# The last group's sums over heads on two engines, p of the places on ScalarE, and the list of units among the one-hots

## The chip, the core and the metric

The kernel runs on one core of a Trainium2 chip. The metric is the device time of one execution in microseconds; the time of a kernel is the median of several executions. Engines are named as in the profile: PE (TensorE), DVE (VectorE), ACT (ScalarE), POOL (GpSimd) and SP, whose queue only issues transfers here.

## The reference

There are N = 6250 nodes with D = 256 features, 4 heads of 64 channels, 8 experts. The edges' sources and destinations come as `src` and `dst`; only the first N edges matter, because node n uses edge n.

```python
h = layernorm(x)
xt = (h @ weight).reshape(-1, 4, 64)
alpha = softmax(leaky_relu(al(xt[src]) + ar(xt[dst]), 0.01), axis=1)   # over the 4 heads
tmp = einsum('nh,nhd->nd', alpha[:N], xt[dst[:N]])                     # sum over heads
x = x + tile(tmp, 4)                                                   # the same 64 values for each head
tokens = layernorm(x)
probs = softmax(tokens @ router_w.T); the two largest, normalised to sum 1
for e in range(8):
    y = gelu(tokens @ w1[e] + b1[e]) @ w2[e] + b2[e]
    moe = tokens + sum of combine[:, e] * y
out = x + moe
```

## The kernel before

Nodes are laid on 128 partitions in NT = 49 tiles and worked on in five groups of 10, 10, 9, 10 and 10 tiles. For each group the kernel gathers the destinations' rows (`gather`, on POOL's queue), turns them on PE, multiplies them with the folded weights (`features`: 293 columns for each node, that is 4 heads of 72 columns, of which 64 are features and 8 are the heads' products with the router's rows), looks up the sources' terms (`look_up`), and makes the attention weights alpha (`attend_1`, `exponents`, `attend_2`).

`attend_3` is the sum over heads: a product of the 4 x 72 columns with alpha, an addition of two heads to the other two, and an addition of those two, the last one into the row of `xs[g]` that will be stored to a table in DRAM. `route` then takes the 8 router products, finds the best two experts of each node, stores the group's rows to the table (L605, SP's queue) and writes which of the 28 pairs of experts each node has (`mine_all`). `rank` and `ranked` count, on PE and DVE, the nodes of the same pair ahead of each node. For the first four groups these steps are spread by `tasks` between the matmuls of the next group; for the last group there is no next one, and they stand one after another.

After the last group follows a stage without loop. DVE adds up the counts (`ends`, `starts`, `base`), multiplies them out (`ms`) and gets each node's place in the order of pairs (`place_i`), split into a slice of 128 places and a lane in it (`slice_b`, `lane_b`). One-hot tables of both (`of_slice`, `of_lane`) and two weighted copies of the first (`by[:, 0]` with the partition number p, `by[:, 1]` with the tile number) go to 49 matmuls that sum into `pi`: for each place, which node stands there. This is done in three pieces of 10, 14 and 26 tiles (the 50th is padding). Then comes the list of units: a unit is an expert's work on a slice. `edge`, `has`, `member`, `takes`, `upto` and `every` find which experts each slice needs, a matmul `pu` numbers them, `unit` and `is_unit` make a one-hot of the numbers, and 16 matmuls `pf` make lists of slice and expert, from which the engines load registers (`which`, `for_act`, `for_pe`, `for_dve`). `held_by`, made from `pi`, says which rows the gathers from the table fetch (`fetch`, L939, POOL's queue). `keep_on` is a row of 26 matmuls whose result is not used.

The expert loop follows: 125 units, for each a load of w1 (`fill`), the first product (`first`, L1117), a gelu on ACT, the second product (`second`, L1133) and two additions into `acc` on DVE, with the layernorms (`norm`), transposes (`turn_slice`) and scattered stores of finished slices (`finish`) among them.

Each engine works through its instructions in program order, and the program is written out in the order in which they are to stand. Tiles of the pool `work` named with the tag `pxs` share two buffers in turn: the five groups' `pxs`, then `ms`, then `by`.

Of the kernel before, what the change touches and what calls it, by code (L numbers as in the profile page):

```python
# [9 lines left out]
FP = mybir.dt.float32  # L10
BF = mybir.dt.bfloat16
I32 = mybir.dt.int32
AF = mybir.ActivationFunctionType
ALU = mybir.AluOpType
# [8 lines left out]
def kernel(  # L23
# [37 lines left out]
    nc = tc.nc  # L61
    N, D = x.shape
    H, OC = attn_l.shape
    NE, _, F = w1.shape
    P = 128
    NT = -(-N // P)
# [17 lines left out]
    NPAIR = len(PATH)  # L84
    TS = 128
    NS = -(-N // TS)
# [3 lines left out]
    HB = OC + NE  # L90
    AR = H * HB
# [5 lines left out]
    U = D  # L97
# [11 lines left out]
    held = early.enter_context(tc.tile_pool(name="held", bufs=1))  # L109
# [4 lines left out]
    def wide(v, n):  # L114
        return v.rearrange("p (t k) -> p t k", k=1).to_broadcast([v.shape[0], v.shape[1], n])

    def long(v, n):
        return v.rearrange("p (t k) -> p t k", t=1).to_broadcast([v.shape[0], n, v.shape[1]])
# [12 lines left out]
    number = const.tile([128, 1], FP, name="number")  # L131
# [7 lines left out]
    xs = [held.tile([P, n, R], FP, name=f"x{g}") for g, (_, n) in enumerate(GROUPS)]  # L139
# [18 lines left out]
    mine_all = held.tile([P, NT, NPAIR], BF, name="mine_all")  # L158
    rank_all = held.tile([P, NT], FP, name="rank_all")
    outside = held.tile([P, 1], FP, name="outside")  # L160

    NTE = NT + NT % 2
    high_1 = held.tile([P, NTE * P], BF, name="high_1")
# [14 lines left out]
    work = early.enter_context(tc.tile_pool(name="work", bufs=2))  # L178
    small = early.enter_context(tc.tile_pool(name="small", bufs=2))
# [39 lines left out]
    for of, pattern, k in ((count_up, [[1, 128]], 0), (number, [[0, 1]], 1)):  # L219
        nc.gpsimd.iota(  # L220
            of, pattern=pattern, base=0, channel_multiplier=k,
# [160 lines left out]
    def pair_tables():  # L382

        nc.vector.tensor_scalar(before_b, count_up, number, None, ALU.is_gt)
        nc.vector.tensor_scalar(huge_b, ident, -HUGE, None, ALU.mult)
        nc.vector.tensor_scalar(valid, number, float(LAST), None, ALU.is_lt)

        nc.vector.tensor_scalar(
            outside, number, float(LAST), float(2 * NS * TS), ALU.is_ge, ALU.mult
        )  # L390


        for e in range(NE):
            nc.vector.memset(order[:, e : e + 1], 2.0 ** (NE - e))


        one_of = first_pool.tile([P, 2, NPAIR], FP, name="one_of")
        for i, (a, b) in enumerate(PATH):
            for k, e in enumerate((a, b)):
                nc.vector.memset(one_of[:, k, i : i + 1], float(e))  # L400
        for i, (a, b) in enumerate(PATH):
            nc.vector.memset(pairs[:, i : i + 1], 2.0 ** (NE - a) + 2.0 ** (NE - b))

        other = small.tile([NS, NE, NPAIR], FP, name="other", tag="mr", bufs=1)
        for k, to in enumerate((member, other)):
            nc.vector.tensor_tensor(
                to,
                one_of[:NS, k : k + 1, :].to_broadcast([NS, NE, NPAIR]),
                wide(count_up[:NS, :NE], NPAIR),
                ALU.is_equal,  # L410
            )
        nc.vector.tensor_tensor(member, member, other, ALU.add)

    def statistics(of, t0, n):
        stats = small.tile([P, n, 6], FP, name="stats", bufs=1)
        mv = small.tile([P, n, 2], FP, name="mv")
        for i in range(n):
            nc.vector.bn_stats(stats[:, i, :], of(t0 + i))
        for i in range(n):
            nc.vector.bn_aggr(mv[:, i, :], stats[:, i, :])  # L420
        return mv
# [52 lines left out]
    pxss, sqs, rstd_ds = {}, {}, {}  # L474
# [66 lines left out]
    def attend_2(g):  # L541

        ex, n = exs.pop(g), GROUPS[g][1]
        s = tiny("s", n)
        nc.vector.tensor_reduce(s, ex, AX.X, ALU.add)
        nc.vector.reciprocal(s, s)
        nc.vector.tensor_tensor(s, s, rstd_ds.pop(g), ALU.mult)
        alpha = small.tile([P, n, H], FP, name="alpha")
        nc.vector.tensor_tensor(alpha, ex, wide(s, H), ALU.mult)
        exs[g] = alpha  # L550

    def attend_3(g, i, n):

        at = slice(i, i + n)
        v = pxss[g][:, at, :AR].rearrange("p t (h k) -> p t h k", k=HB)
        nc.vector.tensor_tensor(
            v, v,
            exs[g][:, at, :].rearrange("p t (h k) -> p t h k", k=1)
            .to_broadcast([P, n, H, HB]), ALU.mult,
        )  # L560
        nc.vector.tensor_tensor(v[:, :, 0:2, :], v[:, :, 0:2, :], v[:, :, 2:4, :], ALU.add)
        nc.vector.tensor_tensor(
            xs[g][:, at, U : U + HB], v[:, :, 0, :], v[:, :, 1, :], ALU.add
        )


# [88 lines left out]
    def paced(t, n, of):  # L655

        nc.gpsimd.tensor_copy(pace[: of.shape[0]], of)
        for i in range(t, min(t + n, NT)):
            gather(i)

    fillers = {
        1: weights_columns,
        2: pair_tables,
        7: lambda: nc.vector.tensor_tensor(
            low_0[:, :NT, :], long(count_up[:, :NT], NT), wide(low, NT), ALU.not_equal
# [72 lines left out]
    def tasks(g):  # L738

        n = GROUPS[g][1]  # L740
        at = {i: [] for i in range(n)}

        def put(i, what):
            at[min(i, n - 1)].append(what)

        if g >= 1:
            f = g - 1
            m = GROUPS[f][1]
            put(1, lambda: attend_1(f))
            put(2, lambda: exponents(f))  # L750
            put(2, lambda: attend_2(f))
            for i in range(0, m, 3):
                put(3 + i // 3, lambda i=i: attend_3(f, i, min(3, m - i)))
            steps = route(f)
            for i in range(5):
                put(7 + i // 2, lambda: next(steps))
        if g >= 2:
            f2 = g - 2
            put(1, lambda: rank(f2))
            put(2, lambda: ranked(f2))  # L760
        if g == 3:
            put(0, load_experts)
        if g == 4:
            put(0, load_biases)
        return at

    at = {}
    for k, (g, b, n) in enumerate(FEATURES):
        if b == 0:
            at = tasks(g)  # L770
        after = None
        for j in range(n):
            i = b + j
            features(g, i, blocks, j)
            t = GROUPS[g][0] + i
# [19 lines left out]
    z = NG - 1  # L795
    n = GROUPS[z][1]
# [2 lines left out]
    rank(z - 1)  # L799
    ranked(z - 1)  # L800
    attend_2(z)
    attend_3(z, 0, n)
    steps = route(z)
    for _ in steps:
        pass
# [18 lines left out]
    nc.vector.tensor_tensor(starts, ends, count, ALU.subtract)  # L824
    base = small.tile([P, NG, NPAIR], FP, name="base", bufs=1)
    nc.vector.tensor_tensor(base, counts[:, :NG, :], long(starts, NG), ALU.add)
    ms = work.tile([P, NT, NPAIR], FP, name="ms", tag="pxs")
    for g in range(NG):
        nc.vector.tensor_tensor(
            ms[:, group(g), :], mine_all[:, group(g), :],  # L830
# [17 lines left out]
    slice_b, lane_b = parts  # L848

    pi = ps.tile([TS, 2, NS], FP, name="pi", tag="px")  # L850
    of_lane = held.tile([P, TS, NTE], BF, name="of_lane", tag="high_1")
    of_slice = held.tile([P, NS, NTE], BF, name="of_slice", tag="low_0")
    by = work.tile([P, 2, NS, NTE], BF, name="by", tag="pxs")

    for t0, t1 in ((0, 10), (10, 24), (24, NTE)):
        at, n = slice(t0, t1), t1 - t0
        for to, k, of in ((of_lane, TS, lane_b), (of_slice, NS, slice_b)):
            nc.vector.tensor_tensor(
                to[:, :, at], steps_b[:, :k, :n], long(of[:, at], k), ALU.is_equal
            )  # L860
        nc.vector.tensor_scalar(
            by[:, 0, :, at], of_slice[:, :, at], number, None, ALU.mult
        )
        nc.vector.tensor_tensor(
            by[:, 1, :, at], of_slice[:, :, at], long(count_b[:, at], NS), ALU.mult
        )
        for t in range(t0, min(t1, NT)):
            nc.tensor.matmul(
                pi, of_lane[:, :, t], by[:, :, :, t], start=(t == 0), stop=(t == NT - 1)
            )  # L870

    edge = small.tile([NS, 2], FP, name="edge", bufs=1)
    for k in range(2):
        nc.vector.tensor_scalar(
            edge[:, k : k + 1], number[:NS], float(TS), float(k * TS), ALU.mult, ALU.add
        )
    has = small.tile([NS, NPAIR], FP, name="has", bufs=1)
    nc.vector.tensor_scalar(has, ends[:NS], edge[:, 0:1], None, ALU.is_gt)
    nc.vector.scalar_tensor_tensor(
# [11 lines left out]
    nc.vector.tensor_copy(every, upto[:, NE - 1 :])  # L891
    pu = ps.tile([NS, 1], FP, name="pu", tag="r")
    nc.tensor.matmul(pu, before_b[:NS, :NS], every, start=True, stop=True)


    fields = small.tile([NS, 2, NE], BF, name="fields", bufs=1)
# [270 lines left out]
    for u in range(NU + LAG + 1):  # L1167
# [11 lines left out]
        k, step = divmod(u, 4)  # L1179
# [46 lines left out]
```

## Time and profile before

| | us |
|---|---|
| median of 3 executions | 432.43 (431.76 to 432.58) |
| the profiled execution | 430.84 |
| its span in the trace | 429.1 |
| PE busy in the span | 368.8 |
| DVE busy | 312.5 |
| ACT busy | 226.0 |
| POOL busy | 199.9 |

A line of the timeline gives the start and the duration in us, the engine, the line of the kernel, the operation, the tile written and the tiles read, their sizes (partitions x elements for each partition) and how many instructions were merged; in brackets stands the idle time of the engine ahead of it and what ended it. A line of groups gives the total busy time and the mean in ns after the first bar. "POOLq" or "SPq" is an engine's queue of commands. In the page's rows over the span, a digit is the busy share of one fortieth of the span in tenths, and PEclk the clock that PE was granted in the same unit.

### The profile page before, as it was taken

How to read it: one execution, taken by the hardware profiler on the slowest of the kernel's cores; microseconds unless marked ns; L12 is line 12 of the kernel's file. 1: busy time of each engine (PE TensorE's matmuls, PEld its weight loads, DVE VectorE, ACT ScalarE, POOL GpSimd, SP SyncE). 2: the span in 40 equal slices, each digit the busy share in tenths (PEclk: the TensorE clock that was granted, in tenths of full speed). 3: DMA queues.
4: the chain of work that ended last, by engine and by line, in shares of the span. 5: the costliest groups of instructions: out<-in, count | busy, mean ns of one | idle time of the engine just before them, and what ended most of it. 6: DMA issues, size and time to landing. Idle time of an engine off the chain costs nothing.

```text
span 429.1 us, 9886 instructions
## 1 busy us (share of the span) xinstructions
PE 368.8 (86%) x2575; PEld 320.0 (75%) x2575; DVE 312.5 (73%) x1092; ACT 226.0 (53%) x658; POOL 199.9 (47%) x240
## 2 busy tenths in 40 slices
PE   5798599888992127979999999999999999999990
PEld 4676388777881115469999999999998899999990
DVE  5999525897988896548778778877876877555551
ACT  3486279575762000057666666667665666333330
POOL 0068888888202000573343567667656633233222
PEclk9699699999997555799999999999999999999997
DMA  7974232446663110766667677777777765666610
GB/s 218 354 236 135 74 105 73 162 168 191 210 227 162 80 80 0 215 185 164 196 178 197 188 233 219 212 224 235 216 217 196 202 192 180 190 186 186 177 69 23
DMA packets 53896, 74.63 MB, mean 174 GB/s; under 512 B 7686, under 2 KB 48250, under 8 KB 52948
## 3 DMA queue, kind: packets, MB, share of 16 engines
q1 hardware_dynamic: 46028, 52.45, 39.9%
q0 software_dynamic: 7248, 21.29, 16.6%
q8 instruction: 23, 0.38, 0.4%
q10 hardware_dynamic: 568, 0.27, 0.3%
q14 instruction: 29, 0.24, 0.2%
HBM read 59.13 MB, written 14.87 MB: 172 GB/s over the span
## 4 chain that ended last, share of the span: by engine, by line
PE 49%; POOL 2%; issue 2%; ACT 1%; DVE 1%; POOLq 0%; ACTq 0%; DVEq 0%
PE ph L1117 24%; PE py L1133 23%; PE pt L1063 2%; POOL xr L939 1%; POOL nm L1020 1%; ACT hid L1124 0%; POOLq L1221 0%; DVE acc L1140 0%; DVE stats L1014 0%; ACT tok L1030 0%; ACTq L1077 0%; ACT acc L1040 0%; POOL out_dram L1144 0%; ACT tokT L1064 0%; POOL mv L1019 0%
## 5 line engine op out<-in xcount | busy, mean ns | idle before, releaser
L1117 PEld LDWEIGHTS ph<-tokT,w 128*128 128x128 f32 x1000 | 130.2, 191 | 13.8 <-ACT tokT L1064 7.7
L1117 PE MATMUL ph<-tokT,w 128*128 (+1 forms) x1000 | 132.5, 276 | 4.8 <-ACT tokT L1064 4.6
L1133 PE MATMUL py<-big,hid 128*128 x500 | 128.6, 380 | 0.0
L1124 ACT ACTIVATE hid<-ph,b_cols 128x128 f32<-128x128 f32 x250 | 77.9, 363 | 75.4 <-PE ph L1117 74.2
L1133 PEld LDWEIGHTS py<-big,hid 128*128 128x128 f32 x500 | 85.4, 191 | 7.0 <-DVE acc L1140 0.2
L939 POOL DMA_INDIRECT xr<-table,held_by x49 | 49.6, 1013 | 72.7 <-DVE held_by L913 39.2
L1140 DVE SCALAR_TENSOR_TENSOR acc<-py,shares,acc 128x256 f32 (+1 forms) x125 | 60.5, 484 | 28.0 <-PE py L1133 17.3
L1144 POOL DMA_INDIRECT out_dram<-acc,held_out x49 | 50.9, 1038 | 55.4 <-DVE acc L1140 39.2
L1140 DVE SCALAR_TENSOR_TENSOR acc<-big,shares,acc (+1 forms) x125 | 60.2, 481 | 11.3 <-issue 6.1
L1030 ACT ACTIVATE tok<-xr,nm 128x256 f32<-128x256 f32 x49 | 29.3, 599 | 60.9 <-DMA w<-in_L_ffn_w_dram 42.2
L480 PE MATMUL px<-w_sb,tT 128*128 128x293 f32 x196 | 56.6, 420 | 0.0
L480 PEld LDWEIGHTS px<-w_sb,tT 128*128 128x128 f32 x196 | 35.0, 194 | 7.3 <-issue 0.3
L236 POOL DMA_INDIRECT big<-in_x_dram,dst_sb x31 | 34.3, 1107 | 7.2 <-issue 6.8
L488 ACT COPY pxs<-px 128x293 f32<-128x293 f32 x49 | 19.8, 404 | 27.6 <-PE px L480 25.3
L251 ACT COPY tT<-pt 128x512 f32<-128x512 f32 (+2 forms) x56 | 26.9, 527 | 9.3 <-PE pt L247 8.9
L1004 DVE TENSOR_TENSOR xr<-xr 128x512 f32<-128x512 f32 (+1 forms) x25 | 17.2, 688 | 17.0 <-issue 17.0
L1040 ACT ACTIVATE acc<-xr,nm 128x256 f32<-128x256 f32 x49 | 29.1, 597 | 0.0
L509 PE MATMUL pl<-al_sb,high 128*128 128x196 bf16 x147 | 19.4, 250 | 8.0 <-DVE al_sb L464 5.9
L509 PEld LDWEIGHTS <-high 128*128 128x128 bf16 x147 | 13.6, 98 | 13.8 <-issue 6.1
L517 DVE TENSOR_REDUCE ag<-pl 128x8 f32<-128x392 f32 (+1 forms) x25 | 13.8, 551 | 11.8 <-PE pl L513 11.8
L1019 POOL TENSOR_SCALAR mv<-mv 128x2 f32<-128x2 f32 (+1 forms) x25 | 5.7, 229 | 35.0 <-DVE mv L1016 33.3
L236 POOL DMA_INDIRECT xd_own<-in_x_dram,dst_sb x18 | 18.5, 1027 | 4.4 <-issue 2.7
(217 smaller groups left out, 478.2 us busy)
## 6 DMA issues: line engine op xcount, KB each, us to landing
w<-in_L_ffn_w_dram SPq DMA_DIRECT2D x125, 256.0 KB
table<-x SPq DMA_DIRECT2D x4, 1685.0 KB
x<-in_x_dram SPq DMA_DIRECT2D x10, 512.0 KB
big<-in_L_ffn_w_dram SPq DMA_DIRECT2D x2, 1024.0 KB
high<-highs SPq DMA_DIRECT2D x1, 1568.0 KB
table<-x SPq DMA_DIRECT2D x1, 1516.5 KB
big<-in_L_ffn_b_dram SPq DMA_DIRECT2D x1, 1024.0 KB
xr<-table,held_by POOLq DMA_INDIRECT x49
```

The lines of the kernel that those rows point to most:

```text
L236: nc.gpsimd.indirect_dma_start(out=xd(t), out_offset=None, in_=x[:, :], in_offset=bass.IndirectOffsetOnAxis(ap=dst_sb[:, t : t + 1], axis=0),)
L251: nc.scalar.copy(tT, pt)
L480: nc.tensor.matmul(px, blocks[c][:, k * P : (k + 1) * P], w_sb[:, c, :], start=(c == 0), stop=(c == DC - 1),)
L509: nc.tensor.matmul(pl[:, k, :, :], high_1[:, t * P : (t + 1) * P], al_sb[:, part, :, :], start=(part == 0), stop=False,)
L939: nc.gpsimd.indirect_dma_start(out=xr[:, i, :], out_offset=None, in_=table[:, :], in_offset=bass.IndirectOffsetOnAxis(ap=held_by[:, s0 + i ...
L1030: nc.scalar.activation(tok[:, i, :], xr[:, i, :D], AF.Identity, bias=bias[:, i : i + 1], scale=scale[:, i : i + 1],)
L1040: nc.scalar.activation(acc[:, s * D : (s + 1) * D], xr[:, i, :D], AF.Identity, bias=bias[:, i : i + 1], scale=more[:, i : i + 1],)
L1117: nc.tensor.matmul(ph[:, j, :], w[:, c * F + j * 128 : c * F + (j + 1) * 128], tokT[:, bass.ds(rows_at + c * TS, TS)], start=(c == 0), sto ...
L1124: nc.scalar.activation(hid[:, j, :], ph[:, j, :], AF.Gelu, bias=b1_cols[:, :, j][:, bass.ds(at_act[u][0], 1)])
L1133: nc.tensor.matmul(py, hid[:, j, :], we2[:, j, bass.ds(at_pe[u][1], D)], start=(j == 0), stop=(j == FC - 1),)
L1140: nc.vector.scalar_tensor_tensor(to, y, share, to, op0=ALU.mult, op1=ALU.add)
L1144: nc.gpsimd.indirect_dma_start(out=ends_at[s][:, :], out_offset=bass.IndirectOffsetOnAxis(ap=held_out[:n, s : s + 1], axis=0), in_=acc[:n, ...
```

## The change

There are four edits. The last group's sums over heads are made in two parts: the 8 columns of router products on DVE, and then the 64 feature columns on GpSimd, with the same three operations each. `by[:, 0]` is made by an ACT instruction in place of a DVE one, and `of_slice` is made ahead of `of_lane`. The pieces of the one-hots are 8, 16 and 26 tiles; the list of units from `has` to the matmul `pu` stands between the second and the third piece, in place of behind the third. The two `edge` instructions move into `pair_tables`, near the start of the kernel, and `ms` gets the buffer of `x1` (group 1's rows), so that `by` takes the buffer that `ms` had and the last group's `pxs` stays in place.

```diff
-    def attend_3(g, i, n):
+    def attend_3(g, i, n, engine=nc.vector, k0=0, k1=HB):
         at = slice(i, i + n)
-        v = pxss[g][:, at, :AR].rearrange("p t (h k) -> p t h k", k=HB)
-        nc.vector.tensor_tensor(
+        v = pxss[g][:, at, :AR].rearrange("p t (h k) -> p t h k", k=HB)[:, :, :, k0:k1]
+        engine.tensor_tensor(
             v, v,
             exs[g][:, at, :].rearrange("p t (h k) -> p t h k", k=1)
-            .to_broadcast([P, n, H, HB]), ALU.mult,
-        )
-        nc.vector.tensor_tensor(v[:, :, 0:2, :], v[:, :, 0:2, :], v[:, :, 2:4, :], ALU.add)
-        nc.vector.tensor_tensor(
-            xs[g][:, at, U : U + HB], v[:, :, 0, :], v[:, :, 1, :], ALU.add
+            .to_broadcast([P, n, H, k1 - k0]), ALU.mult,
+        )
+        engine.tensor_tensor(v[:, :, 0:2, :], v[:, :, 0:2, :], v[:, :, 2:4, :], ALU.add)
+        engine.tensor_tensor(
+            xs[g][:, at, U + k0 : U + k1], v[:, :, 0, :], v[:, :, 1, :], ALU.add
         )
...
     attend_2(z)
-    attend_3(z, 0, n)
+    attend_3(z, 0, n, nc.vector, OC, HB)
+    attend_3(z, 0, n, nc.gpsimd, 0, OC)
     steps = route(z)
...
-    ms = work.tile([P, NT, NPAIR], FP, name="ms", tag="pxs")
+    ms = held.tile([P, NT, NPAIR], FP, name="ms", tag="x1")
...
-    for t0, t1 in ((0, 10), (10, 24), (24, NTE)):
+    def places(t0, t1):
         at, n = slice(t0, t1), t1 - t0
-        for to, k, of in ((of_lane, TS, lane_b), (of_slice, NS, slice_b)):
+        for to, k, of in ((of_slice, NS, slice_b), (of_lane, TS, lane_b)):
             nc.vector.tensor_tensor(
                 to[:, :, at], steps_b[:, :k, :n], long(of[:, at], k), ALU.is_equal
             )
-        nc.vector.tensor_scalar(
-            by[:, 0, :, at], of_slice[:, :, at], number, None, ALU.mult
-        )
+        nc.scalar.activation(by[:, 0, :, at], of_slice[:, :, at], AF.Identity, scale=number)
...
-    edge = small.tile([NS, 2], FP, name="edge", bufs=1)
-    for k in range(2):
-        nc.vector.tensor_scalar(
-            edge[:, k : k + 1], number[:NS], float(TS), float(k * TS), ALU.mult, ALU.add
-        )
+    places(0, 8)
+    places(8, 24)
     has = small.tile([NS, NPAIR], FP, name="has", bufs=1)
...
     nc.tensor.matmul(pu, before_b[:NS, :NS], every, start=True, stop=True)
+    places(24, NTE)
```

More of the change, by code (lines that the diff above doesn't have):

```diff
@@ L160 @@
     outside = held.tile([P, 1], FP, name="outside")
+    edge = held.tile([NS, 2], FP, name="edge")
     NTE = NT + NT % 2
@@ L412, in pair_tables @@
         nc.vector.tensor_tensor(member, member, other, ALU.add)
+        for k in range(2):
+            nc.vector.tensor_scalar(
+                edge[:, k : k + 1], number[:NS], float(TS), float(k * TS), ALU.mult, ALU.add
+            )
     def statistics(of, t0, n):
```

## The prediction

> **What bounds the kernel now.** I read the page first (where each engine is busy over the span), then the timeline between 138 and 182 us, which is the stage that the change touches, then the waits of that stage, and last the timeline around the few GpSimd instructions that read SBUF.
>
> ```profile
> DVE  5999525897988896548778778877876877555551
> POOL 0068888888202000573343567667656633233222
> PEclk9699699999997555799999999999999999999997
> DMA  7974232446663110766667677777777765666610
> ```
>
> One digit is 10.7 us. In slices 13 to 16 (139 to 182 us) the PE clock is at a half, GpSimd's row is empty, and the only full row is DVE's: the serial routing stage between the projections and the expert loop. In the busy times by stage PE is busy 108.00 us of the 108.00 between 192 and 300, and 114.81 of 116 after that, so the loop has no room: a microsecond won or lost before it goes into the span whole. The stage itself, from the timeline:
>
> ```profile
> 138.22 0.20 DVE L549 TENSOR_TENSOR alpha<-ex,s 128x40 f32<-128x40 f32 x1
> 138.45 3.16 DVE L556 TENSOR_TENSOR pxs<-pxs,alpha 128x2880 f32<-128x2880 f32 x1
> 141.65 1.66 DVE L561 TENSOR_TENSOR pxs<-pxs 128x1440 f32<-128x1440 f32 x1
> 143.34 0.91 DVE L562 TENSOR_TENSOR x<-pxs 128x720 f32<-128x720 f32 x1
> 144.29 0.24 DVE L588 TENSOR_TENSOR logits<-own_r,x 128x80 f32<-128x80 f32 x1
> ...
> 164.45 4.82 PE L868 MATMUL pi<-by,of_lane 128*128 128x98 bf16 x25 [1.07 <-DVE edge L874]
> ...
> 169.20 0.20 PE L893 MATMUL pu<-every,before_b 49*49 49x1 bf16 x1
> 169.44 0.23 DVE L903 TENSOR_SCALAR unit<-upto,pu 49x8 f32<-49x8 f32 x1 [2.81 <-PE pu L893]
> ...
> 169.90 1.19 DVE L908 TENSOR_TENSOR is_unit<-count_up,unit 49x1000 bf16<-49x1000 f32 x1
> 171.02 0.19 DVE L912 COPY part_of<-pi 128x49 f32<-128x49 f32 x1
> ...
> 171.24 0.21 DVE L913 SCALAR_TENSOR_TENSOR held_by<-part_of,pi 128x49 int32<-128x49 f32 x1
> 171.74 1.11 POOL L939 DMA_INDIRECT xr<-table,held_by  x1 [39.17 <-DVE held_by L913]
> ```
>
> The reader is to see one chain: the three sums over heads (138.45 to 144.29 = 5.84 us, all on DVE), routing and ranks, the one-hots of places (156.41 to 164.45), 25 matmuls `pi`, then `pu`, `unit`, `is_unit`, `held_by`, and the first gather. GpSimd waited 39.2 us for that gather.
>
> **The change part by part.**
>
> *Sums over heads.* DVE keeps 8 of 72 columns: 320, 160 and 80 elements instead of 2880, 1440 and 720. The 128x288, 128x144 and 128x72 rows of the same lines took 0.45, 0.31 and 0.24 us, the large ones add 1.04 ns per element; so 0.49 + 0.33 + 0.24, and with 0.03 to 0.04 between them 1.17 us. Taken alone this makes the logits 4.67 us earlier.
>
> GpSimd gets 2560, 1280 and 640 elements, 4480 in all. No row of the trace shows GpSimd streaming two inputs. The nearest row writes only:
>
> ```profile
> L722 POOL IOTA steps_b<- 128x3328 bf16 x1 | 5.2, 5244 | 0.0
> ```
>
> 1.58 ns per element, so 7.1 us, is the low end. The Trainium skill ("GPSIMD Engine Reference", section 3.1) gives 4497 ns for exactly this operation at 2048 fp32 elements, 2.20 ns per element, because both inputs take turns at one read port: 5.62 + 2.81 + 1.41 = 9.8 us, an estimate. I take 9.8, since the iota reads nothing, and a fifth more (11.8) as the high end for the rows of 64. Nobody but the store of the last group's table (L605) reads its result. That store went out at 147.57 and DMA traffic was over by 153 us, so it takes some 5 us; the gather that reads the table is at 171.74. Ending at 149 to 151, GpSimd delays no transfer. Behind it in its own queue are only the gathers, and behind the store in SP's queue the w1 loads of 175.61.
>
> *The port.* What decides is whether DVE can run beside it. The trace has one clear case of both reading SBUF:
>
> ```profile
> 73.53 1.13 DVE L556 TENSOR_TENSOR pxs<-pxs,alpha 128x864 f32<-128x864 f32 x1
> ...
> 74.16 0.54 POOL L657 COPY pace<-pxs 128x1 f32<-128x1 f32 x1
> ...
> 130.59 1.98 POOL L472 TENSOR_TENSOR rstd_d<-sq,minus_half 128x10 f32<-128x10 f32 x1
> 130.66 0.24 DVE L588 TENSOR_TENSOR logits<-own_r,x 128x80 f32<-128x80 f32 x1
> ```
>
> A GpSimd copy of one element, elsewhere 0.18 to 0.21 us, took 0.54 and ended at 74.70, 0.04 after the DVE product with two SBUF inputs (74.66): it was locked out until that ended. The other two lines say that DVE was not held by a 1.98 us GpSimd power; but that reads only 10 elements and computes the rest of the time. The Trainium skill ("SBUF — State Buffer", section "Who interferes with whom") speaks against this change: a DVE instruction with two SBUF inputs and a GpSimd instruction that reads SBUF exclude each other for the whole instruction, and the first to issue wins. By the first row alone (DVE has precedence) the change loses nothing on DVE; by the rule DVE waits out each of three long GpSimd instructions. Both fit the copy. I take the rule: GpSimd's reads here last as long as the instruction.
>
> By the rule: DVE's product runs 138.45 to 138.94; GpSimd's product then holds the port to 144.6; DVE's first addition 0.33 (to 145.0 with the hand-over); GpSimd's addition to 147.85; DVE's second 0.24 (148.2); GpSimd's third to 149.6; the logits, which also have two SBUF inputs, at 149.7. That is 5.4 us later than 144.29, where 4.67 earlier was wanted. DVE is blocked for about 9.8 us, all of it on the chain. With 7.1 us of GpSimd it is +2.7, with 11.8 +7.4.
>
> *ScalarE makes by[:,0].* DVE loses three L861 instructions; they were followed by the next after 0.27, 0.32 and 0.48 us: 1.07 us off the chain. ScalarE gets Identity over 392, 784 and 1274 elements. An Identity of 256 took 0.599 (L1030); the copies of L251 and L1064 grew 0.83 to 0.87 ns per element, so 0.7, 1.05 and 1.45 us. Each starts when `of_slice` is there (now made before `of_lane`), and DVE still has `of_lane` and by[:,1] to make, 1.0, 1.7 and 2.6 us: hidden, at worst 0.3 us (bounds 0 and 0.4, the latter if all 256-element costs scaled). ScalarE had nothing between 138.65 and the load of the expert list, so nobody is delayed behind these three.
>
> *List of units among the one-hots.* From L878 to `every` (164.49 to 166.40) were 1.91 us hidden under the 25 matmuls. They now stand ahead of the last third of the one-hots: +1.91 on the chain. In return `pu`, `unit` and `is_unit` (169.20 to 171.02) go under those matmuls. From the first one-hot: chunks of 8 and 16 take 1.17 and 2.09 us (slope 0.52 ns per element of the L858 rows, fewer instructions), the list 1.91, the chunk of 26 0.74 + 1.80 + 0.81; PE begins its 25 at +8.56, where it was +8.04, and ends at +13.4 instead of +12.86; `held_by` ends at +13.9 instead of +15.04 (1.16 gained), `pf` starts at +13.4 instead of +14.74 (1.34 gained). `for_pe` and the w1 loads hang on the second, so I take 1.3 us. PE is idle before its chunks as before; keep_on starts earlier by the same 1.3 us.
>
> *Two `edge` instructions* go into the DVE queue at 27 us, which is full there, and PE waits for `al_sb` behind it: 0.2 us lost (bounds 0 and 0.2). The end where they stood is in the 1.3. *ms* in the buffer of x1 waits for the table store of group 1, over since about 105 us: nothing.
>
> **Sum.** +5.4 (sums over heads, with the port) − 1.3 (places and list) + 0.2 (edge) = +4.3 us. Against the profiled execution, 430.84 (span 429.1), that is 435.1; that run was 1.6 under the median 432.43, so for the median 436.7.
>
> **The rivals.**
>
> *DVE is not held up (slower turns into faster).* Place: the same port between 138.9 and 149. If DVE takes precedence, or the two share it word by word without loss, the logits come 4.67 us earlier: −4.67 − 1.3 + 0.2 = −5.8, 426.6 us. For it: the copy at 74.16 shows DVE winning, and DVE was never seen to wait. Against: there DVE issued first, and no long GpSimd read was under way. It decides where DVE's waiting adds up to less than 5.8 us of GpSimd's 9.8.
>
> *GpSimd is starved.* DVE has precedence and GpSimd only gets what is left: between 139.6 and 151.7 DVE's two-input instructions leave about 5.4 us, the one-hots almost nothing, so the sums would end at about 164 and the store land at 169. The first gather (165.6 if all else were early) would wait to 168.8, but its rows were not needed before L1004 at 178.11 (172.3 when early): about −5, 427.4 us.
>
> *Half and half.* Instructions share, DVE loses some 3 us: −2.8, 429.6 us.
>
> *PE cools.* If keep_on's 26 matmuls finish early because PE has been busy without a gap and the clock falls again before the first transpose, the first units run at half clock: 1 us more in each case.
>
> **How the numbers follow.** Exclusive port 0.68; DVE undisturbed 0.17; starved 0.06; shared 0.09. The port's case has its own range 433.8 to 438.8 (+1.6 to +6.3: 7.1 and 11.8 us of GpSimd). For 8 in 10 the range must reach the cases of the other sign: 426.4 to 438.8. A measurement of this kernel tells about 0.2%, 0.9 us, from no change. Sharing can end on either side, I split its 0.09 into 0.05 faster, 0.03 within and 0.01 slower. Slower over 0.2%: 0.68 + 0.01 = 0.69; within: 0.03; faster: 0.17 + 0.06 + 0.05 = 0.28.
>
> **What would show it.** Right: between alpha and logits DVE's additions of 160 and 80 elements are recorded at several us each, or idle with GpSimd beside them, and the logits start some 11 us after alpha; three GpSimd rows of about 5.6, 2.8 and 1.4 us; `pu` done before the last `pi`, `held_by` some 13.9 us after the first one-hot. Wrong: logits at 1.2 us after alpha, or GpSimd rows under 3 us for the product, or GpSimd rows that stretch past the one-hots.

## The result, and the profile after

| | before | after |
|---|---|---|
| median of 20 executions, us | 432.62 (431.08 to 434.61) | 434.34 (432.71 to 435.61) |
| ratio to before | | 1.0032, 95% interval 1.0019 to 1.0046 |
| profiled execution, us | 430.84 | 433.74 |
| its span, us | 429.1 | 432.0 |

The changed kernel is slower by 0.32% of 432.62, 1.4 us (0.8 to 2.0). The forecast was 4.3 us slower. The page shows the stage, in the rows over the span:

```profile
DVE  4899615987988988448788779777976877555551
POOL 0058888888202800553444376667666643322222
PEclk9999699999997555699999999999999999999997
```

GpSimd's slice at 140 to 151 us (the 14th) has gone from 0 to 8, beside a DVE that is still full. The timeline of that slice (start and duration in us) says with what:

```profile
139.66 0.20 DVE L555 TENSOR_TENSOR alpha<-ex,s 128x40 f32<-128x40 f32 x1
...
139.90 0.49 DVE L563 TENSOR_TENSOR pxs<-pxs,alpha 128x320 f32<-128x320 f32 x1
139.94 4.80 POOL L563 TENSOR_TENSOR pxs<-pxs,alpha 128x2560 f32<-128x2560 f32 x1 [5.91 <-DVE alpha L555]
140.43 4.51 DVE L568 TENSOR_TENSOR pxs<-pxs 128x160 f32<-128x160 f32 x1
144.83 2.91 POOL L568 TENSOR_TENSOR pxs<-pxs 128x1280 f32<-128x1280 f32 x1
144.97 2.86 DVE L569 TENSOR_TENSOR x<-pxs 128x80 f32<-128x80 f32 x1
147.81 1.55 POOL L569 TENSOR_TENSOR x<-pxs 128x640 f32<-128x640 f32 x1
147.86 1.59 DVE L595 TENSOR_TENSOR logits<-own_r,x 128x80 f32<-128x80 f32 x1
149.49 0.23 DVE L597 TENSOR_REDUCE m<-logits 128x10 f32<-128x80 f32 x1
```

DVE's three instructions behind its product each end just after the GpSimd instruction beside them: 144.94 after 144.74, 147.83 after 147.74, 149.45 after 149.36. An addition of 160 elements is recorded at 4.51 us; the waiting is inside the record, no idle time is shown. Behind DVE's product, which had issued first and took its usual 0.49 us, only the reduction at 149.49 is not stretched, and it starts when GpSimd is done. GpSimd's three stand behind DVE's three in the program, so DVE's two additions cannot be waiting for a result of theirs. The place of the list, further down the same timeline:

```profile
167.69 0.20 PE L899 MATMUL pu<-every,before_b 49*49 49x1 bf16 x1
...
169.75 4.87 PE L876 MATMUL pi<-by,of_lane 128*128 128x98 bf16 x25 [1.86 <-DVE by L872]
...
170.22 1.19 DVE L915 TENSOR_TENSOR is_unit<-count_up,unit 49x1000 bf16<-49x1000 f32 x1
174.55 1.84 PE L961 MATMUL pf<-is_unit,fields 49*1 49x125 bf16 x16
174.66 0.21 DVE L919 COPY part_of<-pi 128x49 f32<-128x49 f32 x1 [3.25 <-PE pi L876]
174.91 0.21 DVE L920 SCALAR_TENSOR_TENSOR held_by<-part_of,pi 128x49 int32<-128x49 f32 x1
```

`pu` and `is_unit` are now beside or ahead of the last 25 matmuls, as written, and DVE waits 3.25 us for these matmuls with nothing to do.

Counted from the start of alpha, so that the load phase ahead of it drops out, the stage compares as follows (us, from the starts in each timeline). Beside the lines shown so far it takes, before:

```profile
144.56 0.24 DVE L590 TENSOR_REDUCE m<-logits 128x10 f32<-128x80 f32 x1
...
156.41 0.83 DVE L858 TENSOR_TENSOR of_lane<-steps_b,part 128x1280 bf16<-128x1280 bf16 x1
...
173.02 0.47 DVE L961 TENSOR_SCALAR which<-pf 1x125 f32<-1x125 f32 x2 [1.57 <-PE pf L954]
```

and after:

```profile
161.21 0.35 DVE L868 TENSOR_TENSOR of_slice<-steps_b,part 128x392 bf16<-128x392 bf16 x1
...
176.43 0.47 DVE L968 TENSOR_SCALAR which<-pf 1x125 f32<-1x125 f32 x2 [1.31 <-PE pf L961]
```

| | before | after | all sums on DVE | split alone |
|---|---|---|---|---|
| alpha to the reduction behind the logits | 6.34 | 9.83 | 6.34 | 9.82 |
| from there to the first one-hot | 11.85 | 11.72 | 11.73 | 11.84 |
| first one-hot to the list (`which`) | 16.61 | 15.22 | 15.21 | 16.61 |
| sum: alpha to `which` | 34.80 | 36.77 | 33.28 | 38.27 |

The last two columns are the first two experiments. The change is +3.49 us for the split of the sums and −1.52 for the rest, +1.97 together, which is the upper end of what was timed. In the profiled pair alpha itself stands 1.44 us later after the change, but a lag of 0.98 to 1.58 us is there at 16 to 18 us already, ahead of any edit (`edge` is at 28 us). In three later runs whose program is that of the changed kernel up to alpha, it stands at 138.66, 138.71 and 140.17 us. So the lag is taken for the difference between two executions and not for the change.

### The profile page after: what moved, and what is told of

It reads as the page before. It is cut to its first block, busy times and chain, and to the rows that moved or that the text cites. A ratio compares the mean times of both kernels' runs of the same rounds, so it can differ in the third digit from the quotient of the medians.

```text
span 432.0 us, 9890 instructions
## 1 busy us (share of the span) xinstructions
PE 370.5 (86%) x2575; PEld 321.8 (74%) x2575; DVE 314.8 (73%) x1089; ACT 229.4 (53%) x661; POOL 209.1 (48%) x243
## 4 chain that ended last, share of the span: by engine, by line
PE 47%; DVE 2%; issue 2%; POOL 2%; ACT 1%; POOLq 0%; ACTq 0%; DVEq 0%
PE ph L1124 23%; PE py L1140 22%; PE pt L1070 2%; DVE acc L1147 1%; POOL nm L1027 1%; DVE stats L1021 0%; ACT hid L1131 0%; POOL xr L946 0%; POOLq L1228 0%; ACT acc L1047 0%; DVEq L1084 0%; ACT tokT L1071 0%; ACTq L1084 0%; POOL out_dram L1151 0%; POOL mv L1026 0%
## 5 line engine op out<-in xcount | busy, mean ns | idle before, releaser
L1011 DVE TENSOR_TENSOR xr<-xr 128x512 f32<-128x512 f32 (+1 forms) x25 | 17.3, 691 | 16.7 <-issue 16.7
```

## The experiments

The first four ran on a chip on which the kernel before took 445.53 us (median of 47), the later ones where it took 432.9 and 432.1. Each is compared with the kernel before on its own chip. The runs for which no ratio is given were executed once, and only their timelines are read.

**All sums on DVE.**

```diff
-    attend_3(z, 0, n, nc.vector, OC, HB)
-    attend_3(z, 0, n, nc.gpsimd, 0, OC)
+    attend_3(z, 0, n)
```

> The changed kernel with the last group's sums over heads back on DVE; the other edits stay. If the port is what the change lost by, the other edits alone gain 1.3 to 1.5 us less 0 to 0.2 for edge: 1.1 to 1.5 us faster than before, ratio 0.997. The rival, that the places and the list lose time and the sums gain, expects it slower than before.

Measured: ratio 0.9964 (0.9943 to 0.9986), 1.6 us faster than before; the table shows 1.52. The other edits gain what they were written for, and the rival, that they lose time, is out.

```profile
169.55 0.35 DVE L867 TENSOR_TENSOR of_slice<-steps_b,part 128x392 bf16<-128x392 bf16 x1
...
184.76 0.47 DVE L967 TENSOR_SCALAR which<-pf 1x125 f32<-1x125 f32 x2 [1.31 <-PE pf L960]
```

**The split alone**, in the kernel before, with the buffer of `ms` moved.

> The kernel before with only the split of the sums (and the buffer of ms that it needs). The trace after shows the logits 3.5 us later counted from alpha: 3.3 to 3.7 us slower, ratio 1.008. By my prediction's sum it would be 5.4 us slower; by the rival without a lock 4.7 us faster.

Measured: ratio 1.0077 (1.0052 to 1.0103), 3.4 us slower; 3.47 in the table. The two parts of the change add up, and the loss is the split's.

```profile
148.53 0.20 DVE L549 TENSOR_TENSOR alpha<-ex,s 128x40 f32<-128x40 f32 x1
...
149.29 4.50 DVE L562 TENSOR_TENSOR pxs<-pxs 128x160 f32<-128x160 f32 x1
...
153.83 2.87 DVE L563 TENSOR_TENSOR x<-pxs 128x80 f32<-128x80 f32 x1
...
158.35 0.23 DVE L591 TENSOR_REDUCE m<-logits 128x10 f32<-128x80 f32 x1
```

**GpSimd that writes and doesn't read.**

```diff
-    attend_3(z, 0, n, nc.gpsimd, 0, OC)
+    v = pxss[z][:, :, :AR].rearrange("p t (h k) -> p t h k", k=HB)[:, :, :, :OC]
+    for of in (v, v[:, :, 0:2, :], xs[z][:, :, U : U + OC]):
+        nc.gpsimd.memset(of, 0.0)
```

> The changed kernel with GpSimd's three instructions replaced by three memsets of the same three regions, which read nothing; the 64 feature columns of the last group are left out of the result. If DVE is held up by GpSimd's reads, DVE's additions go back to 0.33 and 0.24 us and the kernel is 5.8 to 6.2 us faster than before, ratio 0.986. If any GpSimd instruction on SBUF holds DVE, its additions are still stretched by the length of the memsets, some 4 to 7 us in all, and the ratio is near 1.0.

Measured: ratio 0.9892 (0.9856 to 0.9929), 4.8 us faster (3.2 to 6.4); alpha to `which` is 28.61, 6.2 less than before. The memsets do not wait for alpha and ran some 6 us ahead of the place that I had meant, beside the fourth group's routing. In the timelines of GpSimd and of DVE:

```profile
143.81 3.49 POOL L813 MEMSET pxs<- 128x2560 f32 x2
...
144.49 0.24 DVE L607 TENSOR_TENSOR rest<-rest,x 128x80 f32<-128x80 f32 x1
144.77 0.24 DVE L585 SCALAR_TENSOR_TENSOR eq<-rest,order 128x80 f32<-128x80 f32 x1
```

There too DVE instructions with two SBUF inputs run at their 0.24 us, beside 3.5 us of GpSimd writing. These memsets hold nobody. Behind alpha, with no GpSimd instruction left, DVE's two additions take 0.33 and 0.24 us; so the run also shows what the stage would have been had DVE been free: 1.68 us from alpha to the reduction instead of 9.83.

**DVE instructions with one SBUF input beside GpSimd's product.**

```diff
+    attend_3(z, 0, n, nc.gpsimd, 0, OC)
...
+    of = mine_all[:, :10, :]
+    for _ in range(4):
+        nc.vector.tensor_reduce(aside_n, of, AX.X, ALU.add)
+    nc.vector.tensor_copy(aside[:, :128], count_up)
+    nc.vector.tensor_reduce(aside_n, of, AX.X, ALU.add)
     attend_3(z, 0, n, nc.vector, OC, HB)
-    attend_3(z, 0, n, nc.gpsimd, 0, OC)
```

> The changed kernel with GpSimd's sums issued first, and on DVE four reductions of 280 elements (one SBUF input), a copy of 128 fp32 elements, and a fifth reduction ahead of DVE's part; these six write aside. If only a second SBUF input goes through the shared port, the four reductions take 0.45 us each beside GpSimd's product. If the copy uses both ports it is held until the product ends, and the product itself is not longer than 4.3 us because nobody is ahead of it. If DVE is held by any instruction, the first reduction takes some 4 us.

```profile
149.62 1.88 DVE L815 TENSOR_REDUCE aside_n<-mine_all 128x10 f32<-128x280 bf16 x4
...
149.78 4.50 POOL L563 TENSOR_TENSOR pxs<-pxs,alpha 128x2560 f32<-128x2560 f32 x1 [5.92 <-DVE alpha L555]
151.41 2.95 DVE L816 COPY aside<-count_up 128x128 f32<-128x128 f32 x1
154.29 0.43 DVE L817 TENSOR_REDUCE aside_n<-mine_all 128x10 f32<-128x280 bf16 x1
154.36 2.90 POOL L568 TENSOR_TENSOR pxs<-pxs 128x1280 f32<-128x1280 f32 x1
154.64 2.97 DVE L563 TENSOR_TENSOR pxs<-pxs,alpha 128x320 f32<-128x320 f32 x1
```

The reductions run at 0.47 us each while GpSimd reads; a copy of 128 fp32 elements takes 2.95 and ends at 154.36, 0.08 after the product; the next product with two inputs is held through GpSimd's addition (to 157.61, after 157.26). What is held goes by the kind of DVE instruction, not by its size: those with two SBUF inputs, and this fp32 copy from SBUF to SBUF (the only one that was tried); the bf16 reductions are free. The product itself took 4.50 where nobody was ahead of it, a little more than the expected 4.3.

**Why the product was quicker than I took it: a dense operand.** The product's second operand is replaced by its first.

```diff
-            exs[g][:, at, :].rearrange("p t (h k) -> p t h k", k=1)
+            v if engine is nc.gpsimd else exs[g][:, at, :].rearrange("p t (h k) -> p t h k", k=1)
             .to_broadcast([P, n, H, k1 - k0]), ALU.mult,
```

> The changed kernel with the second operand of GpSimd's product replaced by the product's own tile, so that both inputs are full tensors of 2560 elements; the last group's features come out as sums of squares. If the product was quicker than I took it (4.3 us for 5.62) because alpha is one value repeated 64 times, this product takes 5.4 to 5.7 us after DVE's first product ends, and the logits come 1.1 to 1.4 us later than in the changed kernel, some 9.4 us after alpha. If a product is simply quicker than an addition on GpSimd, it stays at 4.3 us.

Measured: 4.45 us. The product no longer waited for alpha and ran at 134.05, beside the fourth group's routing, where it held a DVE instruction of 80 elements for 4.43 us; what I expected of the logits can therefore not be read. But the rate can: with a full tile as second input it is the same, so the repeated alpha is not needed for it.

```profile
134.05 4.45 POOL L563 TENSOR_TENSOR pxs<-pxs 128x2560 f32<-128x2560 f32 x1
134.17 4.43 DVE L603 SCALAR_TENSOR_TENSOR rest<-x,logits 128x80 f32<-128x80 f32 x1
138.58 2.91 POOL L568 TENSOR_TENSOR pxs<-pxs 128x1280 f32<-128x1280 f32 x1
138.63 0.24 DVE L606 TENSOR_REDUCE x<-rest 128x10 f32<-128x80 f32 x1
138.91 2.68 DVE L607 TENSOR_TENSOR rest<-rest,x 128x80 f32<-128x80 f32 x1
```

These lines settle more than the rate. The DVE instructions belong to the fourth group and share no tile with GpSimd's product and addition, so a wait for data is out as the cause of the stretching. And an fp32 reduction runs at its 0.24 us inside GpSimd's addition, between two instructions with two inputs that are held.

**The same, an addition for the product.**

```diff
-            .to_broadcast([P, n, H, k1 - k0]), ALU.mult,
+            .to_broadcast([P, n, H, k1 - k0]), ALU.add if engine is nc.gpsimd else ALU.mult,
```

> The changed kernel with GpSimd's product turned into an addition of alpha (same operands, same sizes; the last group's features come out wrong). If GpSimd's cost follows the operation, the first instruction takes 5.4 to 5.8 us from the end of DVE's first product (2.2 ns per element, as its additions of 1280 and 640 elements do) and the logits start 1.2 us later. If it follows the size or the access pattern, it stays at 4.3 us.

Measured: 4.80 us from its start, the same as the product, of which 0.44 behind DVE.

```profile
138.94 4.80 POOL L563 TENSOR_TENSOR pxs<-pxs,alpha 128x2560 f32<-128x2560 f32 x1 [5.92 <-DVE alpha L555]
139.42 4.51 DVE L568 TENSOR_TENSOR pxs<-pxs 128x160 f32<-128x160 f32 x1
```

The operation is not the reason either. A fixed time for each instruction does not explain it: the changed kernel's two additions (2.91 us for 1280 elements, 1.55 for 640, from their starts) lie on 2.1 ns per element and 0.2 us, which would make 5.6 us of 2560. What is left is the access pattern or some other effect of the size: the instructions at 1.7 ns per element read one tile together with a repeated value or with itself, those at 2.2 to 2.4 read two different regions of a tile. No run varied that alone, so it stays open.

**Places without ScalarE.** The sums and by[:,0] both on DVE.

```diff
-        nc.scalar.activation(by[:, 0, :, at], of_slice[:, :, at], AF.Identity, scale=number)
+        nc.vector.tensor_scalar(by[:, 0, :, at], of_slice[:, :, at], number, None, ALU.mult)
```

> The changed kernel with the sums over heads on DVE and by[:,0] on DVE too, so that only the list, the pieces and edge stay of the change. By my working ScalarE's three instructions are worth 1.07 us on the chain: from the first one-hot to the list of experts 16.3 us, against 15.2 in the changed kernel and 16.6 in the one before. If the order of the list alone is the gain, it stays at 15.2.

Measured: first one-hot to `which` 16.20 us. So ScalarE is worth 0.98 of the 1.39 us, and the order of the list with its pieces, `edge` out of the way, 0.41.

**A version that beats both: ScalarE for the products.**

```diff
-    attend_3(z, 0, n, nc.gpsimd, 0, OC)
...
+    for i in range(n):
+        for h in range(H):
+            nc.scalar.activation(
+                feats[:, i, h, :], feats[:, i, h, :], AF.Identity, scale=exs[z][:, i, h : h + 1]
+            )
...
     rank(z)
+    add_heads(0, 4)
     ranked(z)
...
+    add_heads(4, 6)
+    nc.sync.dma_start(table_v[:, group(z), :], xs[z])
     places(0, 8)
```

`feats` are the 64 feature columns of the last group's `pxs`, and `add_heads(i, m)` is DVE's two additions over the heads for m tiles from tile i on. Not shown: the store of this group inside `route` is left out, and `warm` moves ahead of the products.

> The changed kernel with GpSimd's part replaced: ScalarE makes the 40 products of 64 columns (one for each tile and head), DVE adds 4 tiles where it waits for PE's ranks and 6 tiles ahead of the one-hots, and the table store of the group goes out after these. If the port is what cost the time, ScalarE beside DVE holds nobody: DVE spends 1.17 + about 1.5 us on the chain where it spent 5.84 before, with the other edits 4.5 to 5 us faster than before, ratio 0.989. If the product by ScalarE is late (40 instructions at 0.3 us or more, past the one-hots), the gain shrinks to 2 us or less.

Measured: 427.37 us, ratio 0.9879 (0.9852 to 0.9905) to the kernel before, 5.2 us faster (4.1 to 6.4). Its timeline:

```profile
138.71 0.20 DVE L555 TENSOR_TENSOR alpha<-ex,s 128x40 f32<-128x40 f32 x1
...
139.05 9.64 ACT L817 ACTIVATE pxs<-pxs,alpha 128x64 f32<-128x64 f32 x40
139.47 0.33 DVE L568 TENSOR_TENSOR pxs<-pxs 128x160 f32<-128x160 f32 x1
139.83 0.24 DVE L569 TENSOR_TENSOR x<-pxs 128x80 f32<-128x80 f32 x1
...
144.12 0.68 DVE L823 TENSOR_TENSOR pxs<-pxs 128x512 f32<-128x512 f32 x1
144.83 0.43 DVE L824 TENSOR_TENSOR x<-pxs 128x256 f32<-128x256 f32 x1
145.72 0.18 DVE L645 TENSOR_TENSOR counts<-counts,rank 128x28 f32<-128x28 f32 x1 [0.46 <-PE rank L637]
```

Forty ScalarE instructions take 9.64 us, about as long as GpSimd's three (9.42), and in the same place. DVE's additions of 160 and 80 elements are back at 0.33 and 0.24 us. The sums of four tiles fit into DVE's wait for the ranks (1.51 us before, 0.46 left). Alpha to `which` is 30.07 us, against 34.80 before and 36.77 after the change.

## Why the prediction was right and wrong

The likeliest case was the right one, and its mechanism is what the trace and the experiments show: DVE's instructions with two SBUF inputs wait out GpSimd's, one after another, on the chain. The rule that it was taken from, of the Trainium skill ("SBUF — State Buffer", section "Who interferes with whom"), agrees with this trace in all three instructions, with the memsets (writes only, not held) and with the reductions (one input, not held). The size was wrong, +1.4 us (0.8 to 2.0) for +4.3. The step that failed is one term of the sum: the sums over heads with the port, taken as +5.4 us, measured +3.49. That is 1.9 of the 2.1 us between what the forecast had for this stage (+4.1, as `edge` is not in it) and its +1.97; the other 0.2 is of the places and the list. Inside the term two things were mis-sized:

- *GpSimd's product*, 5.62 us in the sum, took 4.35 (140.39, when DVE's product was done, to 144.74): −1.3. The 2.20 ns per element of the Trainium skill ("GPSIMD Engine Reference", section 3.1) were measured on an addition, and not on "exactly this operation" as I wrote. They fit the first addition here (2.80 us for 1280 from 144.94 on, 2.19 ns; the second took 1.53 for 640, 2.4 ns) but not the product, 1.70 ns. Why the product is quicker stays open. The low end that I had from the iota row, 1.58 ns, was nearer, and I set it aside because the iota reads nothing.
- *Hand-overs.* I counted the held instruction's full time after each release (0.33, 0.24), some 0.1 us around each, and then the logits' own time. In fact a held instruction ends 0.09 to 0.20 us after the release, and GpSimd's next one starts 0.07 to 0.09 us after its last. The logits, 0.24 us alone, ended 0.09 after GpSimd. That, less the 0.2 us that GpSimd's two additions took beyond my estimate, is the other −0.6.

The other terms and claims:

- *ScalarE, the pieces and the list*: −1.3 foreseen, −1.52 measured. From the first one-hot PE's 25 matmuls began at +8.54 (worked out: +8.56), ended at +13.41 (+13.4), `pf` began at +13.34 (+13.4), `held_by` ended at +13.91 (+13.9). ScalarE's instructions took 0.63, 0.96 and 1.36 us (0.7, 1.05, 1.45) and were hidden. That −1.39 met −1.3 is in part luck: ScalarE gave 0.98 for my 1.07, the list 0.41 for the 0.27 that were left of 1.34. The other 0.13 was not foreseen and lies ahead of the first one-hot: `of_lane` read the cast just ahead of it and started 0.04 us after its end, while `of_slice`, now first, reads an earlier one and starts 0.09 us before that end.
- *edge*: 0.2 us were put down; with all sums on DVE the time is 1.6 us below before, where the table has 1.52. No loss is seen in the time, where 0.2 us is within the interval; in the profiled pair DVE's lag grows from 0.97 to 1.10 us across the two instructions.
- *Nothing downstream*: the store of the table, moved behind GpSimd in the program, delayed no gather, and from the first DVE instruction of the layernorms (L1004 before, L1011 after) to the end it is 250.99 us before and 250.49 after; 250.26 to 250.89 in the four runs of the later chips.
- *PE does not cool*: the granted clock is 1.00 from 184 to 210 us in both profiles, and the first 16 matmuls of `first` take 2.05 us in both.

Of the rivals, the undisturbed DVE and the starved GpSimd are out: GpSimd waited only 0.45 us behind DVE's first product, and 0.11 and 0.02 behind the two additions. So is an even sharing of the port: three times DVE's instruction ended only after GpSimd's, however few elements it had.

Two slips of the prediction change nothing in this. In the last of its slices 13 to 16 (172 to 182 us) PEclk is 7, and DVE and GpSimd are both at 5, so what it says of them holds for the first three. And the range of its port case begins at 433.8 us, where +1.6 on 432.43 makes 434.0.

## What to carry to other kernels

Work that was moved from VectorE to GpSimd did not run beside VectorE here, because GpSimd's instructions stream from SBUF and VectorE's next instructions have two SBUF inputs: the elements cost 1.04 ns each on VectorE and 1.7 to 2.4 on GpSimd, and VectorE waited all the same. Before moving work, look at what VectorE does meanwhile (in these runs, with two inputs or in the fp32 copy it waited, in a reduction it didn't), and try ScalarE first, which held nobody here. In these traces the mark of such a wait is a small instruction that is stretched to the length of GpSimd's, with no idle time ahead of it.

## What the hardware showed that I had not expected

A GpSimd instruction that streams 2560 fp32 elements at two inputs took 4.35 to 4.50 us (1.70 to 1.76 ns per element) whether it multiplied or added and whether its second input was a repeated value or a full tile, while its first addition of two different regions took 2.80 for 1280. And a VectorE instruction that was held ended sooner after the release than it takes alone, by nearly the same amount at every size: 0.09 us for 0.24 (80 elements), 0.20 for 0.33 (160), and, in the run with the reductions, 0.35 for 0.49 (320), that is 0.13 to 0.15 us less. Presumably that much of its fixed time passes while it waits, which no run here separates.
